# SS2D softplus in a four-layer network: the sum of its two parts moved from GpSimd to TensorE and ScalarE

## The chip, the cores and the metric

The kernel runs on one core of a Trainium2 chip. The time is the device time of one execution in microseconds; the median over several runs counts. The engines are TensorE (PE, with its weight loads as PEld), VectorE (DVE), ScalarE (ACT), GpSimd (POOL) and SyncE (SP), whose queue issues most DMAs.

## The reference

The input is an image batch of 8 x 56 x 56 x 128 in float32. Four layers follow one another. Layers 0, 2 and 3 are deformable convolutions with an MLP. Layer 1 is a state-space block (SS2D): layer norm, an input projection to 256 channels and a gate, a depthwise 3 x 3 convolution with SiLU, then a selective scan over the pixels in four directions, whose outputs are summed, normalized, gated, projected back, and followed by an MLP. The part that matters here, cut from the reference:

```python
x_dbl = jnp.einsum('bkdl,kcd->bkcl', xs, x_proj_w)
dts, Bsm, Csm = jnp.split(x_dbl, [R, R + N], axis=2)
dt = jnp.einsum('bkrl,kdr->bkdl', dts, dt_projs_w)
dt = jax.nn.softplus(dt + dt_projs_b[None, :, :, None])
A = -jnp.exp(A_logs).reshape(K, Di, N)
def step(h, t):
    dt_t, u_t, B_t, C_t = t
    h = h * jnp.exp(dt_t[..., None] * A) + (dt_t * u_t)[..., None] * B_t[:, :, None, :]
    y = jnp.einsum('bkdn,bkn->bkd', h, C_t)
    return (h, y)
```

So for each image, each of the K = 4 directions, each of the Di = 256 channels and each of the N = 16 states, a linear recurrence runs over L = 3136 pixels. Its inputs are dt (after softplus), the product dt x u, and the rows B and C that all channels share.

## The kernel before

The whole network is one program. Only the layer `Vss` (SS2D) is touched. It takes 128 steps one after the other: 8 images x 4 directions (in the order 0, 1, 3, 2) x 4 chunks of SC = 784 pixels. Directions 1 and 3 go through the image column by column, so that their views of `xb` and `y` are strided. A step is 32 units; a unit is one scan of 128 partitions (32 channels x 4 states) over 784 pixels: 8 channel groups `cg`, each with 4 state groups `sg`.

*A unit.* ScalarE makes dA = exp(dt x A) into PSUM (`decay`, L1424; two buffers). VectorE makes u = dtu x b (L1434), or, for the last of four state groups, GpSimd makes it as `up` (L1430). VectorE scans (L1537) into one of three buffers h; GpSimd multiplies h by the row c into hc (L1542; six buffers). TensorE sums hc over states into the PSUM tile acc (L1456), and ScalarE copies acc out (L1467) every eight units. ScalarE also keeps the last column of each scan as the next chunk's start (`st`, L1540). `dtu` is one PSUM tile of two banks: TensorE copies dt x u into it by an identity matmul (`spread`, L1418) once for four units, and can do so only when the last u of the four units before has been read by VectorE.

*Preparation of the next step* (`prepare`, L1314) runs beside the units as a Python generator: each `next` emits a bit of it, at two of every four units. It projects xb to dts, B and C (L1324), and for each half h of the 256 channels: a matmul with `dt` (L1337) in two parts of SH = 392 pixels, Abs and Relu on ScalarE (L1338, L1339) into `sp` and `dd[:, 0]`, then Exp and Ln on `sp` (L1341, L1342), since softplus(x) = relu(x) + log(1 + exp(-|x|)). GpSimd adds the two (L1344) and multiplies the sum by xs into `dd[:, 1]` (L1346). SP's queue stores dd to DRAM (L1348), from where `fetch_dt` (L1364) loads it spread over partitions and `fetch_row` (L1357) loads the rows of B and C. `dd` and `sp` have one buffer each.

*The background stages* run the same way, a bit for each unit in which they get a turn: `input_stage` of the next image (whose convolution is nine matmuls into one PSUM tile, L1171, twice for each chunk of 448 pixels) and `output_stage` of finished chunks. They and `prepare` share one PSUM bank, `misc`, a pool with one buffer.

*What sets the order.* The program is emitted unit by unit in Python, and a scheduler then orders each engine's instructions by priority (order of emission) and by when it takes them to be ready. The order is fixed when the program is built; each engine executes its instructions in that order and waits on semaphores.

Of the kernel before, what the change touches and what calls it, by code (L numbers as in the profile page):

```python
# [120 lines left out]
SH = SC // 2  # L121
# [911 lines left out]
class Vss:  # L1033
# [280 lines left out]
    def prepare(self, s, k, c):  # L1314

        nc, w = self.nc, self.w
        xs = self.part(self.xb, k, c)
        dbl = self.prep.tile([XD, SC], F32, name="dbl", tag="dbl")
        s["rows"] = self.dram.tile([NST, 2 * SC], F32, name="rows", tag="rows")
        s["dd"] = self.dram.tile([DI, 2 * SC], F32, name="dds", tag="dds")  # L1320
        for b in range(2):
            ps = self.misc()
            for ch in range(NCH):
                nc.tensor.matmul(ps[:XD, :SH].rearrange("p (a b) -> p a b", b=W), lhsT=w["xproj"][:, ch, k, :], rhs=xs[:, ch, SR // 2 * b : SR // 2 * (b + 1)], start=ch == 0, stop=ch == NCH - 1)  # L1324
            yield
            nc.scalar.copy(dbl[:, SH * b : SH * (b + 1)], ps[:XD, :SH])
        nc.sync.dma_start(out=s["rows"].rearrange("n (x e) -> (n x) e", x=2), in_=dbl[RANK:])
        yield
        for h in range(NCH):
            dd = self.prep.tile([128, 2, SC], F32, name="dd", tag="dd")  # L1330
            sp = self.prep.tile([128, SC], F32, name="sp", tag="sp")

            bias = w["dt_b"][:, NCH * k + h : NCH * k + h + 1]
            for b in range(2):
                at = slice(SH * b, SH * (b + 1))
                ps = self.misc()
                nc.tensor.matmul(ps[:, :SH], lhsT=w["dt"][:, k, 128 * h : 128 * (h + 1)], rhs=dbl[:RANK, at], start=True, stop=True)  # L1337
                nc.scalar.activation(sp[:, at], ps[:, :SH], AF.Abs, bias=bias)  # L1338
                nc.scalar.activation(dd[:, 0, at], ps[:, :SH], AF.Relu, bias=bias)  # L1339
                yield  # L1340
            nc.scalar.activation(sp, sp, AF.Exp, scale=-1.0)  # L1341
            nc.scalar.activation(sp, sp, AF.Ln, bias=1.0)  # L1342
            yield
            nc.gpsimd.tensor_add(dd[:, 0], dd[:, 0], sp)  # L1344
            yield
            nc.gpsimd.tensor_mul(dd[:, 1].rearrange("p (a b) -> p a b", b=W), dd[:, 0].rearrange("p (a b) -> p a b", b=W), xs[:, h])  # L1346
            yield
            nc.sync.dma_start(out=s["dd"][128 * h : 128 * (h + 1)], in_=dd.rearrange("p x e -> p (x e)"))  # L1348
            yield
# [289 lines left out]
```

## Time and profile before

| | |
|---|---|
| median of three runs | 17851.06 us (17844.23 to 17852.9) |
| profiled execution, its own time | 17839.74 us |
| span of the profiled execution | 17838.2 us |
| busy in the span: VectorE | 15386.3 us (86%) |
| TensorE | 13881.5 us (78%) |
| GpSimd | 11758.9 us (66%) |
| ScalarE | 10928.2 us (61%) |
| granted TensorE clock, mean | 0.851 |
| SS2D's scans, first to last | 2218 to 13404 us |
| in that stretch: GpSimd busy | 10437.8 of 11185.8 us |
| VectorE, TensorE, ScalarE | 10146.8, 8894.4, 6900.0 us |

The profile is one execution. Busy time is the union of an engine's instructions; PE's ends are modelled, and one float32 matmul of the program shows as two rows. A line such as "DVE h L1537 <- POOL hc L1542" says that VectorE's instruction of line 1537, which writes h, began after an idle time that ended with GpSimd's instruction of line 1542. "x4096" is a count, and names like hc<-h,c are output<-inputs.

### The profile page before, as it was taken

The page shows a single profiled execution, that of the slowest core. Times are in us where ns is not written, and L with a number is a line of the kernel's source. Part 1 is how long each engine was busy: PE and PEld are TensorE (multiplying, and loading weights), DVE is VectorE, ACT ScalarE, POOL GpSimd, SP SyncE. Part 2 cuts the span into 40 slices and gives each one's busy share as a digit, 9 for nine tenths or more (in the row PEclk, how much of TensorE's full clock was granted, in tenths as well). Part 3 has the DMA queues.
Part 4 walks back from the last instruction along what each step waited for, and adds up shares of the span by engine and source line. Part 5 has one row for each costly group of instructions (what it writes and reads, how often), then busy time and mean ns, then how long its engine had stood idle before and what let it go on. Part 6 is the DMA issues. An engine that isn't in the chain of part 4 may idle for free. (4 is left out here: it accounts for less than half of the span.)

```text
span 17838.2 us, 255485 instructions
## 1 busy us (share of the span) xinstructions
PE 13881.5 (78%) x90058; PEld 6881.4 (39%) x90058; DVE 15386.3 (86%) x17779; ACT 10928.2 (61%) x19607; POOL 11758.9 (66%) x6462
## 2 busy tenths in 40 slices
PE   5777788788788788788778878878776888777777
PEld 3555522232232233232223223223224666555555
DVE  8888488998998998998898899899996888888886
ACT  4666566566566566566666656656554666666666
POOL 2222189998998998998998999899992111122221
PEclk7788898899899899889888888989887888777778
DMA  7777544444343343343444344344434777777777
GB/s 211 211 204 206 165 153 154 172 169 150 143 159 141 139 163 137 139 165 137 143 162 143 137 158 144 140 155 150 148 134 134 199 198 199 196 210 193 209 196 176
DMA packets 1343087, 2961.69 MB, mean 166 GB/s; under 512 B 90960, under 2 KB 893716, under 8 KB 1327420
## 3 DMA queue, kind: packets, MB, share of 16 engines
q1 hardware_dynamic: 1341788, 2945.17, 52.9%
q8 instruction: 718, 11.76, 0.3%
q14 instruction: 581, 4.76, 0.1%
HBM read 2240.63 MB, written 866.92 MB: 174 GB/s over the span
## 5 line engine op out<-in xcount | busy, mean ns | idle before, releaser
L1542 POOL TENSOR_TENSOR hc<-h,c 128x784 f32<-128x784 f32 x4096 | 7539.5, 1874 | 640.9 <-DVE h L1537 387.9
L1537 DVE TENSOR_TENSOR_SCAN h<-dA,st,u 128x784 f32<-128x784 f32 x3072 | 5579.2, 1840 | 438.9 <-ACT dA L1424 243.2
L1424 ACT ACTIVATE dA<-dt,v_A 128x784 f32<-128x784 f32 x4096 | 3741.9, 915 | 842.2 <-DVE h L1537 827.7
L1456 PE MATMUL acc<-hc,v_sum 128*32 128x392 f32 x16384 | 3148.3, 542 | 103.9 <-POOL hc L1542 103.3
L1434 DVE TENSOR_TENSOR u<-dtu,b 128x784 f32<-128x784 f32 x3072 | 2864.6, 957 | 382.5 <-PE dtu L1418 378.4
L1418 PE MATMUL dtu<-dt,ident 128*128 128x392 f32 x4096 | 2028.2, 626 | 1081.9 <-issue 833.4
L760 POOL TENSOR_TENSOR ay<-hat,om 112x756 f32<-112x756 f32 (+2 forms) x192 | 504.6, 2628 | 2848.6 <-ACT hat L751 2309.7
L1537 DVE TENSOR_TENSOR_SCAN h<-dA,st,up 128x784 f32<-128x784 f32 x1024 | 1876.7, 1833 | 232.0 <-POOL hc L1542 208.6
L1430 POOL TENSOR_TENSOR up<-dt,b 128x784 f32<-128x784 f32 x1024 | 1908.1, 1863 | 79.5 <-DVE h L1537 47.1
L845 ACT COPY st<-pt 128x448 f32<-128x448 f32 (+1 forms) x2240 | 1177.4, 542 | 1201.1 <-PE pt L843 1194.6
L812 DVE TENSOR_TENSOR win<-win,patch 112x252 f32 (+2 forms) x3456 | 1686.4, 501 | 132.2 <-POOL win L803 32.5
L1540 ACT COPY st<-h 128x1 f32<-128x1 f32 x3072 | 582.6, 190 | 1985.3 <-DVE h L1537 1976.8
L843 PE MATMUL pt<-ident,sw 112*128 112x112 f32 (+2 forms) x8960 | 1600.6, 308 | 165.6 <-DMA sw<-skew 165.5
L1456 PEld LDWEIGHTS acc<-hc,v_sum 128*32 128x32 f32 x16384 | 762.0, 116 | 2485.3 <-issue 1656.6
L1418 PEld LDWEIGHTS dtu<-dt,ident 128*128 128x128 f32 x4096 | 860.1, 230 | 2150.6 <-issue 1365.5
L803 POOL MEMSET win<- 128x1820 f32 (+2 forms) x384 | 630.0, 1647 | 1298.4 <-DMA skew<-win 1111.2
L859 PE MATMUL yps<-st,xw 128*32 128x48 f32 (+5 forms) x35840 | 1075.2, 244 | 420.7 <-ACT st L845 414.6
L843 PEld LDWEIGHTS pt<-ident,sw 112*128 112x128 f32 (+2 forms) x8960 | 1113.4, 160 | 441.0 <-issue 156.8
L809 DVE TENSOR_TENSOR patch<-ay,hat 112x756 f32<-112x756 f32 (+2 forms) x1152 | 1225.3, 1070 | 39.5 <-POOL ay L760 36.6
L859 PEld LDWEIGHTS yps<-st,xw 128*32 128x32 f32 (+2 forms) x35840 | 754.1, 125 | 849.5 <-ACT st L845 501.0
L749 ACT ACTIVATE hat<-om,taps 112x252 f32<-112x252 f32 x1280 | 758.6, 730 | 277.2 <-DVE patch L809 261.4
L1448 PE MATMUL acc<-y,ident 128*64 128x392 f32 x1536 | 599.1, 780 | 348.6 <-ACT y L1467 269.5
(193 smaller groups left out, 19827.3 us busy)
## 6 DMA issues: line engine op xcount, KB each, us to landing
dt<-dds SPq DMA_DIRECT2D x1024, 784.0 KB
b<-rows SPq DMA_DIRECT2D x512, 392.0 KB
c<-rows SPq DMA_DIRECT2D x512, 392.0 KB
dds<-dd SPq DMA_DIRECT2D x256, 784.0 KB
sw<-skew SPq DMA_DIRECT2D x224, 812.0 KB
sw<-skew SPq DMA_DIRECT2D x224, 672.0 KB
sw<-skew SPq DMA_DIRECT2D x224, 588.0 KB
skew<-win SPq DMA_DIRECT2D x128, 560.0 KB
```

What stands on the lines that cost most here:

```text
L809: nc.vector.tensor_mul(patch[:n], bcast(a, 3, KX), bcast(b, 2, KY))
L812: self.last_add = nc.vector.tensor_add(to, to, patch[:n, NCB * p : NCB * (p + 1)]).ins
L843: last = nc.tensor.transpose(ps[:m, n * g : n * (g + 1)], sw[:n, g, p : p + m], self.net.ident[:n, :n])
L845: nc.scalar.copy(st[:m], ps[:m, : G * n])
L859: self.nc.tensor.matmul(yps[CG * g : CG * (g + 1), t0:t1], lhsT=xw[:m, k + part, CG * g : CG * (g + 1)], rhs=st[:m, at + t0 : at + t1], st ...
L1418: last = nc.tensor.matmul(ps[:, b, :SH], lhsT=self.net.ident, rhs=s["dt", cg][:, 1, SH * b : SH * (b + 1)], start=True, stop=True)
L1424: nc.scalar.activation(da[:, :SC], s["dt", cg][:, 0], AF.Exp, scale=w["A"][:, k, NSG * cg + sg : NSG * cg + sg + 1])
L1430: nc.gpsimd.tensor_mul(u, s["dt", cg][:, 1], s["b", sg])
L1434: nc.vector.tensor_mul(halves[0], s["dtu", cg][:, :, :SH], halves[1])
L1456: nc.tensor.matmul(acc[r : r + TC, :SH], lhsT=w["sum"], rhs=hc[:, SH * b : SH * (b + 1)], start=False, stop=sg == NSG - 1)
L1537: nc.vector.tensor_tensor_scan(hh[:, ::step], dA[:, :SC][:, ::step], u[:, ::step], st[:, t : t + 1], ALU.mult, ALU.add)
L1542: nc.gpsimd.tensor_mul(hc, hh, s["c", sg])
```

## The change

The sum on GpSimd goes. In its place, for each of two parts of 392 pixels, TensorE adds the two tiles in the shared PSUM bank by two matmuls with the identity, and ScalarE copies the sum back over `dd[:, 0]`. The product with xs stays on GpSimd. The number of turns that `prepare` takes is the same: the turn that held the sum now holds the first part, and the second part comes in one turn with the product.

```diff
             nc.scalar.activation(sp, sp, AF.Exp, scale=-1.0)
             nc.scalar.activation(sp, sp, AF.Ln, bias=1.0)
             yield
-            nc.gpsimd.tensor_add(dd[:, 0], dd[:, 0], sp)
-            yield
+            for b in range(2):
+                at = slice(SH * b, SH * (b + 1))
+                ps = self.misc()
+                nc.tensor.matmul(ps[:, :SH], lhsT=self.net.ident, rhs=dd[:, 0, at], start=True, stop=False)
+                nc.tensor.matmul(ps[:, :SH], lhsT=self.net.ident, rhs=sp[:, at], start=False, stop=True)
+                nc.scalar.copy(dd[:, 0, at], ps[:, :SH])
+                if b == 0:
+                    yield
             nc.gpsimd.tensor_mul(dd[:, 1].rearrange("p (a b) -> p a b", b=W), dd[:, 0].rearrange("p (a b) -> p a b", b=W), xs[:, h])
             yield
```

## The prediction

> **What bounds the kernel now.** First the page's busy shares, then the busy time of each engine in stretches of one image, then the waits, then the timeline. The edit stands in the SS2D layer, whose scans run from 2218 to 13404 us of the profiled execution (11186 us); the other layers don't touch it, so the whole-span shares say little. These are six stretches of the third image, cut at first scans of steps: steps 0-2, 3-7, 8-9, 10-11, 12, 13-15 (a step has 32 scans).
>
> ```profile
> core 0: us, PE busy (x) PEld busy (x) DVE busy (x) ACT busy (x) POOL busy (x), PEclk, DMA share, GB/s
> 5040.70:5292.10 251.40, 205.90 (x834) 83.62 (x833) 239.66 (x184) 167.64 (x324) 246.60 (x138) 0.91 0.44 153
> 5292.10:5765.20 473.10, 403.38 (x1327) 140.04 (x1327) 399.42 (x330) 297.14 (x508) 410.11 (x229) 0.93 0.39 138
> 5765.20:5946.50 181.30, 152.83 (x538) 52.98 (x532) 158.77 (x116) 115.94 (x210) 165.59 (x92) 0.87 0.41 144
> 5946.50:6114.60 168.10, 120.33 (x402) 34.17 (x398) 156.38 (x114) 96.23 (x151) 167.79 (x93) 0.83 0.39 140
> 6114.60:6193.20 78.60, 41.98 (x176) 13.53 (x176) 77.53 (x57) 36.98 (x72) 72.83 (x42) 0.83 0.35 126
> 6193.20:6443.70 250.50, 198.27 (x772) 76.37 (x773) 238.75 (x176) 159.41 (x275) 244.48 (x135) 0.90 0.48 172
> ```
>
> Read POOL against the length of the stretch. In the fourth it is busy 167.79 of 168.10 us: POOL sets the time. In the first and last it is at 98%, VectorE at 95%. The fifth step holds none of the removed sums, as the same stretches with the instructions of L1344 alone tell:
>
> ```profile
> 6114.60:6193.20 78.60, 0.00 (x0) 0.83 0.35 126
> ```
>
> It is the shortest, 78.6 us against some 84 a step in the others without convolution, VectorE at 99%. So VectorE's floor is 78 to 80 us a step, and the sums are part of what lies above it. The second stretch is different: it holds the input convolution, takes 94.6 us a step, PE is at 85% and POOL at 87%.
>
> How a sum reaches the scans is seen here: POOL does the sum, two hc, one up, then the product of the preparation, and a scan waits 2.44 us because none of the three h buffers has been read by its hc.
>
> ```profile
> 5974.36 1.91 POOL L1344 TENSOR_TENSOR dd<-dd,sp 128x784 f32<-128x784 f32 x1
> ...
> 5981.67 2.28 POOL L1346 TENSOR_TENSOR dd<-dd,xb 128x784 f32<-128x784 f32 x1
> ...
> 5985.80 1.85 DVE L1537 TENSOR_TENSOR_SCAN h<-dA,st,up 128x784 f32<-128x784 f32 x1 [2.44 <-POOL hc L1542]
> ```
>
> The waits over the whole execution (us in total, times, longest):
>
> ```profile
> DVE u L1434 <- PE dtu L1418: 378.4, 154, 48.6
> DVE h L1537 <- POOL hc L1542: 287.1, 261, 3.4
> DVE h L1537 <- ACT dA L1424: 246.2, 245, 5.0
> POOL dd L1344 <- ACT sp L1342: 15.4, 3, 9.8
> ```
>
> VectorE loses 287 us to POOL, but also 246 to ScalarE and 378 to TensorE (48.6 of it before the scans), the two engines that the change loads.
>
> **The change part by part.** The rows that price it, one operation each (busy, mean ns | idle before):
>
> ```profile
> L1344 POOL TENSOR_TENSOR dd<-dd,sp 128x784 f32<-128x784 f32 x256 | 476.1, 1860 | 34.4 <-DMA b<-rows 19.0 <-ACT sp L1342 15.4
> L1346 POOL TENSOR_TENSOR dd<-dd,xb 128x784 f32<-128x784 f32 x256 | 525.6, 2053 | 10.8
> L1245 ACT COPY yc<-misc 128x392 f32<-128x392 f32 x128 | 61.6, 481 | 72.8 <-PE misc L1244 72.2
> ```
>
> and for one pair of identity matmuls of 128x392, which the trace shows as four rows, at a full and at a lowered clock:
>
> ```profile
> 5961.63 1.58 PE L1418 MATMUL dtu<-dt,ident 128*128 128x392 f32 x4
> 8001.39 2.82 PE L1418 MATMUL dtu<-dt,ident 128*128 128x392 f32 x4
> ```
>
> 1. *Removed from POOL*: 256 x 1.86 = 476 us of work. On the path is only what VectorE waits for: 287 us at most, and nothing if another wait takes its place (the third rival). No such wait stands in the step without preparation, so all of it comes from the preparation's bursts. Sums are 1.86 of 1.86 + 2.05, 47%, of a burst; in proportion 136 us would go. A wait is what a burst leaves over three buffers, so halving the burst takes more than half: between 136 and 287 I take 200. Next late after that: VectorE itself, at 95% in three of the stretches.
>
> 2. *Added to TensorE*: 512 pairs x 1.58 = 809 us (1444 at the lower clock). Where PE is at 53 to 82% it lies in PE's idle time. In the convolution steps it need not: u waits for dtu there (35.1 us in this stretch). The built program's order tells how many can hurt. Between one pair of dtu matmuls and the next, some 10 us, 38 of the 512 new pairs share the interval with three or more convolution taps; 156 stand in steps with a convolution at all. Bounds: 0 (below it only by the clock, weighed further down) and 156 x 1.58 = 246 us; nearest to the crowded intervals, I take 38 x 1.58 = 60. If PE's idle time were gone elsewhere, each of the other 356 would cost its 1.58 too, 562 us.
>
> 3. *Added to ScalarE*: 512 copies of 0.48 (the L1245 row), each waiting 72.2/128 = 0.56 for its matmul: ScalarE is held 1.04 x 512 = 535 us. Behind the copy stand the next dA and, behind that, a scan. ScalarE is at 62% (6900 of 11186 us), and 245 of 4096 dA (6%) came late. Bounds 0 (added work can't gain) and half, 268; with one in eight on the path, twice today's share since ScalarE is fuller, 64 us.
>
> 4. *New wait on POOL*: the product dd x xb now follows ScalarE's second copy; behind it stand hc and up. The sum waited for ScalarE 15.4 us in all. In the built order the second copy stands one or two dA ahead of the scan whose hc follows the product, where Ln stood before the sum. I cost it at nothing, hidden by POOL's backlog; uncovered it is 256 x 1.04 = 266 us of POOL time, still below the 476 taken away, and below nothing is excluded, since a wait can't gain.
>
> 5. *PSUM*: misc is one bank, now taken ten times a step instead of six, and from the dd matmul until the copy. Behind it wait the projections and the background stages, which have slack until the next image; PE in order is the danger, since the second pair waits for the first copy with the next dtu behind it. Counted in 2; its upper end takes this in.
>
> 6. *Moved*: the product of the second half now comes at the end of a step, not some three to six units before it, and its store on SP's queue has up to two row loads behind it. Row loads hold POOL up for 14.3 us in the whole trace. Nothing, up to 128 x 2.05 = 262 us if each product's time went on to the rows. The load of dt for that half comes nine units later.
>
> Sum: -200 + 60 + 64 = -76 us against the profiled execution (17839.7 us, span 17838.2), which lies 11 under the median of the runs, 17851.1. Forecast: 17775.
>
> One rule speaks for more. TensorE's clock follows its load here: 0.83 where PE is busy 53%, 0.93 at 85%. The Trainium skill, "TensorE: Matmul & The Clock Gate", in the part on the HAM clock gate, says that activity is what releases the throttle. By it the added matmuls would lift 0.93 towards 1; of the 7 x 403 us of PE time in convolution steps some 190 would go, an estimate from that page, more than the 60 of step 2, and the sum would be -136: 17715. I stay with the rows, since four dtu rows still took 2.82 us among scans whose mean clock is 0.89.
>
> **The rivals.**
> *TensorE becomes the bound (slower)*: in the convolution steps all 156 pairs come ahead of a dtu that VectorE waits for, +246, and these steps' share of POOL's relief (16.4 of 35.4 us of that wait in the image shown, 46%) is lost: -108. With ScalarE's 64: +202, 18053. For it: 35.1 us of waits for dtu and 85%. Against: the few crowded intervals. It decides once 86 of the 156 are exposed (200 - 64 = 136 us).
> *ScalarE's copies make dA late (slower)*: half of the 535 us: -200 + 60 + 268 = +128, 17979. For it: FIFO behind a copy that waits for PE. Against: ScalarE waits 828 us for scans ahead of dA.
> *POOL's burst still overruns three buffers (same)*: -136 + 60 + 64 = -12, 17839. For it: the product, 2.05, the larger half, stays.
> *Full relief (faster)*: 287 go and the rest is hidden: 17564. For it: the step without preparation, at 78.6. Against: that one has little background work too.
>
> **How the numbers follow.** Chances: forecast 0.40, full relief 0.14, same 0.16, TensorE 0.18, ScalarE 0.12. The forecast's own range, with its terms each a little off, is 17690 to 17815. Within 0.2% (36 us), about what a measurement can tell, lies the third rival alone: faster 0.54, same 0.16, slower 0.30. The range for 8 in 10 goes from full relief to just short of the TensorE case: 17560 to 18030, leaving out half of either end.
>
> **What would show it.** Right: stretches four to six get 2 to 3 us a step shorter with POOL under 96% and VectorE over 96%; the wait of scans for hc falls from 287 towards 90. Step 2 wrong: u's wait for dtu grows by over 150 us, in the convolution steps. Step 3 wrong: the wait for dA grows from 246 past 350. Step 4 wrong: a new row, POOL dd waiting for ScalarE's copy, over 100 us.

## The result and the profile after

The changed kernel takes 17926.12 us (median of six runs, 17919.57 to 17951.31) against 17848.71 us for the kernel before (six runs beside it, 17838.29 to 17857.72). The ratio is 1.0046, with a 95% interval of 1.0033 to 1.0059: slower by 77 us, where 76 us faster was forecast. All of it lies in the SS2D scans: they take 11269 us (2225 to 13494) instead of 11186, that is +83, and the rest of the program keeps its time within 3 us.

The page's first part for the kernel after, busy us of each engine (share of the span) and instructions:

```profile
PE 14492.8 (81%) x92106; PEld 7089.2 (40%) x92106; DVE 15359.4 (86%) x17779; ACT 11180.5 (62%) x20119; POOL 11323.2 (63%) x6206
```

GpSimd lost 436 us of work (11758.9 before), as meant. TensorE gained 611, ScalarE 252. VectorE, which does the scans, has the same work as before and ends later, so it waits more. The waits of the kernel after tell for what (us in total, times, longest):

```profile
DVE u L1440 <- PE dtu L1424: 770.9, 279, 54.1
...
DVE h L1543 <- ACT dA L1430: 206.2, 197, 5.6
...
DVE h L1543 <- POOL hc L1548: 57.2, 48, 3.8
```

The wait for GpSimd's hc fell from 287 to 57 us, the relief that was forecast. The wait for ScalarE's dA fell too, from 246 to 206. But the wait of u for dtu, TensorE's copy of dt x u, doubled from 378 to 771. The three together went from 912 to 1034, +122, and the time rose by 77.

By step, over the six images 1 to 6 (counted from 0), the dtu wait grew by 53 us an image: 25 in steps 3 to 6 and 4 in step 7, where the convolution runs, but also 12 in steps 0 to 2 and 12 in steps 13 to 15, where it doesn't. In steps 8 to 12 it stayed as it was, and there the relief shows: the wait for hc fell by 13.

The same six stretches of the third image as before (steps 0-2, 3-7, 8-9, 10-11, 12, 13-15), in the kernel after:

```profile
core 0: us, PE busy (x) PEld busy (x) DVE busy (x) ACT busy (x) POOL busy (x), PEclk, DMA share, GB/s
5084.30:5339.50 255.20, 221.29 (x869) 84.17 (x869) 240.50 (x191) 174.89 (x341) 234.48 (x131) 0.97 0.43 151
5339.50:5828.40 488.90, 439.67 (x1410) 155.02 (x1411) 397.77 (x322) 309.10 (x524) 395.78 (x221) 0.94 0.38 135
5828.40:6002.90 174.50, 154.38 (x581) 54.48 (x580) 158.38 (x117) 117.42 (x212) 156.43 (x86) 0.98 0.40 142
6002.90:6164.70 161.80, 125.77 (x436) 38.56 (x434) 155.70 (x114) 100.29 (x161) 156.95 (x87) 0.87 0.41 147
6164.70:6244.00 79.30, 48.80 (x194) 15.71 (x194) 77.72 (x58) 41.31 (x81) 75.19 (x43) 0.83 0.40 143
6244.00:6498.90 254.90, 209.44 (x807) 79.14 (x807) 238.32 (x175) 161.32 (x283) 233.58 (x129) 0.96 0.47 166
```

Read the lengths against those before. The third and fourth stretch gain 6.8 and 6.3 us. The first two lose 3.8 and 15.8, and the last, which has no convolution, loses 4.4. GpSimd is at 97% in the fourth, where it was at all but 100%, and at 92% in the first and last, where it was at 98%; TensorE is at 87 to 90% in the first three. Over six images the trace gives the same picture, mean us of a step:

| steps of an image | before | after | change, whole group |
|---|---|---|---|
| 0-2 | 84.1 | 85.6 | +4.3 |
| 3-6 | 93.7 | 97.6 | +15.6 |
| 7 | 100.5 | 96.5 | -4.0 |
| 8 | 88.7 | 89.5 | +0.8 |
| 9-11 | 86.1 | 82.4 | -11.0 |
| 12 | 78.7 | 79.4 | +0.7 |
| 13-15 | 83.7 | 85.2 | +4.5 |

That is +10.9 us an image, 87 for eight.

**What a late dtu stands behind.** The timeline of the kernel after shows it. Here, in step 1 of the third image, one half of a dtu copy is done at 5226.34 and the other half, which needs the same dt and the same PSUM tile, 4.4 us later:

```profile
5226.34 0.93 PE L1424 MATMUL dtu<-dt,ident 128*128 128x392 f32 x2 [1.55 <-DVE u L1440]
...
5227.14 1.58 PE L1262 MATMUL misc<-sg,v_outb 128*128 128x392 f32 x4
...
5228.56 1.03 PE L1264 MATMUL misc<-ident,xt 98*128 98x98 f32 x8
...
5229.43 1.51 PE L1266 MATMUL misc<-yin,v_out 128*128 128x392 f32 x4
...
5230.77 0.82 PE L1424 MATMUL dtu<-dt,ident 128*128 128x392 f32 x2
...
5231.63 0.97 DVE L1440 TENSOR_TENSOR u<-dtu,b 128x784 f32<-128x784 f32 x1 [1.61 <-PE dtu L1424]
```

Between the halves TensorE ran sixteen rows of the output stage, and VectorE lost 1.61 us. None of those matmuls is new. TensorE executes its matmuls in the order of the program; the Trainium skill, "TensorE: Matmul & The Clock Gate", in the section on what each phase of a matmul is for, says that only weight loads are pulled ahead and matmuls keep program order. These rows agree: the second half needed nothing that the first had not had, and it ran after the sixteen rows.

The trace can be counted for that. There are 1023 intervals from the end of one dtu copy to the end of the next, 11 us on average. Call one crowded if matmuls other than the copy's own kept TensorE busy for 10 us or more in it:

| | before | after |
|---|---|---|
| crowded intervals | 120 | 179 |
| of them with u waiting for dtu; us waited | 76; 232 | 160; 549 |
| all intervals with u waiting for dtu | 153 | 278 |
| u's wait for dtu within the scans, us | 330 | 717 |

Look at the stretches from the release of the dtu buffer to the late u, 862 us in all before and 1825 after. The new matmuls take just 126 us of TensorE in them. The old ones take more than before: the projection of x (L1324) 187 us for 51, the convolution (L1171) 300 for 168, the sums over states 347 for 187, three lines of the output stage (L1262 to L1266) 182 for 39. Part of that is only that there are more late stretches: for each of them the convolution and the sums take 1.1 and 1.2 us in both kernels, and the projection and the output stage have grown. TensorE stood idle for 36 us of these stretches, 9 of them until one of ScalarE's new copies ended and 1 until a load of dt landed. So neither the copies nor the loads are what dtu waits for there.

**Which intervals became late.** The old matmuls themselves can be followed from one trace to the other: the n-th row of a line and its tiles before is taken for the n-th after. Of 27652 rows within the scans, 4572 run in another interval in the changed kernel. Most of these are of the output stage and the preparation. In no_sum, the kernel below without any sum, 456 do, and sum_back, below, has the order of the changed kernel in all but 26 rows. Sorted by that, u's wait for dtu is, in us:

| intervals of the changed kernel | number | before | after |
|---|---|---|---|
| with a new matmul | 349 | 69 | 170 |
| without one, into which old rows moved | 439 | 85 | 364 |
| with neither | 235 | 175 | 183 |

Of the rise of 387 us, 279 come in intervals that hold no new matmul and got old ones from elsewhere; 101 come in those with the new ones. Where nothing came in, next to nothing changed.

### The profile page after: what moved, and what is told of

Same layout as the page of the kernel before. It is cut to its first block, busy times and chain, and to the rows that moved or that the text cites. A ratio compares the mean times of both kernels' runs of the same rounds, so it can differ in the third digit from the quotient of the medians.

```text
span 17923.7 us, 259791 instructions
## 1 busy us (share of the span) xinstructions
PE 14492.8 (81%) x92106; PEld 7089.2 (40%) x92106; DVE 15359.4 (86%) x17779; ACT 11180.5 (62%) x20119; POOL 11323.2 (63%) x6206
## 5 line engine op out<-in xcount | busy, mean ns | idle before, releaser
L1462 PE MATMUL acc<-hc,v_sum 128*32 128x392 f32 x16384 | 3263.5, 535 | 4.5 <-POOL hc L1548 4.2
L1424 PE MATMUL dtu<-dt,ident 128*128 128x392 f32 x4096 | 1879.0, 577 | 831.3 <-issue 564.3
L1424 PEld LDWEIGHTS dtu<-dt,ident 128*128 128x128 f32 x4096 | 770.2, 208 | 1839.5 <-issue 1031.2
L1171 PE MATMUL misc<-xn,v_tap 128*128 128x448 f32 x2016 | 832.5, 561 | 42.2 <-ACT xn L1208 15.4
```

The lines of the kernel that those rows point to most:

```text
L1424: last = nc.tensor.matmul(ps[:, b, :SH], lhsT=self.net.ident, rhs=s["dt", cg][:, 1, SH * b : SH * (b + 1)], start=True, stop=True)
L1462: nc.tensor.matmul(acc[r : r + TC, :SH], lhsT=w["sum"], rhs=hc[:, SH * b : SH * (b + 1)], start=False, stop=sg == NSG - 1)
```

## The experiments

Each was timed beside the kernel before. The table has the three waits of VectorE from the profiled execution (u for dtu, h for hc, h for dA), their sum, and the time.

| kernel | dtu | hc | dA | sum | median us | ratio to before, 95% |
|---|---|---|---|---|---|---|
| before | 378 | 287 | 246 | 912 | 17849 | |
| after | 771 | 57 | 206 | 1034 | 17926 | 1.0046 [1.0033, 1.0059] |
| no_sum | 363 | 104 | 183 | 649 | 17568 | 0.9845 [0.9828, 0.9861] |
| sum_back | 751 | 265 | 232 | 1248 | 18183 | 1.0193 [1.0176, 1.0210] |
| one_matmul | 714 | 93 | 238 | 1045 | 17954 | 1.0062 [1.0045, 1.0079] |
| pin_after | 801 | 113 | 230 | 1144 | 18012 | 1.0094 [1.0078, 1.0111] |
| hold_only | 622 | 362 | 304 | 1287 | 18205 | 1.0200 [1.0183, 1.0217] |
| work_only | 791 | 135 | 232 | 1158 | 18069 | 1.0124 [1.0107, 1.0141] |
| mixed_k3 | 363 | 210 | 310 | 883 | 17796 | 0.9973 [0.9960, 0.9985] |
| turn_act | 547 | 259 | 159 | 965 | 17879 | 1.0017 [1.0007, 1.0026] |
| slot30_after | 645 | 33 | 227 | 905 | 17828 | 0.9989 [0.9979, 0.9999] |
| slot30_before | 554 | 261 | 328 | 1143 | 18030 | 1.0104 [1.0087, 1.0121] |
| slot30_no_sum | 470 | 44 | 302 | 816 | 17678 | 0.9912 [0.9895, 0.9929] |
| mixed_more | 359 | 197 | 290 | 845 | 17769 | 0.9964 [0.9950, 0.9979] |

The sum of the waits tells the order of the times nearly throughout: +336 us of wait and +336 of time in sum_back, -263 and -279 in no_sum, +375 and +361 in hold_only. So these three waits are where to look.

### The two halves of the change apart

First the relief alone. The sum goes and nothing takes its place; the Ln part of softplus is left out of dd.

```diff
-            for b in range(2):
-                ...
-                nc.scalar.copy(dd[:, 0, at], ps[:, :SH])
-                if b == 0:
-                    yield
+            yield
```

> The sum is left out altogether (dd keeps only the Relu part), so neither GpSimd's sums nor TensorE's pairs nor ScalarE's copies are there: POOL's relief alone. Theory 'crowded intervals' (what costs is PE work queued between two dtu pairs, and the relief itself is real): PE's queue is as before, so the wait of u for dtu stays within 330 to 400 us of its 378, the scans' wait for hc falls from 287 to under 90, time 17550 to 17650. Rival 'freed VectorE' (VectorE, no longer held by POOL, comes to dtu earlier and waits there, with or without new matmuls): the wait for dtu rises by over 150 us and the time is 17750 to 17850.

17568 us. The relief is worth 279 us, more than the 200 taken. Three waits of VectorE in this kernel:

```profile
DVE u L1433 <- PE dtu L1417: 362.5, 138, 44.7
...
DVE h L1536 <- ACT dA L1423: 183.0, 202, 3.7
...
DVE h L1536 <- POOL hc L1541: 103.9, 107, 3.4
```

The wait for hc is 183 us shorter (at 104 it stands a little above the 90 expected), and that for dA 63. The wait for dtu stays where it was before (378), so a faster GpSimd does not bring it on. That disposes of the idea that VectorE, freed, merely runs into TensorE.

Then the added work alone: the change stays, its copies go to a part of dd that the product overwrites, and GpSimd's sum is put back.

```diff
-                nc.scalar.copy(dd[:, 0, at], ps[:, :SH])
+                nc.scalar.copy(dd[:, 1, at], ps[:, :SH])
                 if b == 0:
                     yield
+            nc.gpsimd.tensor_add(dd[:, 0], dd[:, 0], sp)
```

> The changed kernel with GpSimd's sum put back beside the pairs and copies (the copies go to the tile that the product overwrites): all of the added work, no relief. PE's queue order is that of the changed kernel. Theory 'crowded intervals': the wait for dtu stays at 650 to 800 us as in the changed kernel, the scans' wait for hc comes back to 200 to 300, time 18050 to 18200. Rival 'freed VectorE': without relief VectorE comes late to dtu and the wait for dtu is under 550 us, time 17900 to 17980.

18183 us, 336 above before. The waits:

```profile
DVE u L1441 <- PE dtu L1425: 751.1, 263, 53.3
...
DVE h L1544 <- POOL hc L1549: 264.6, 314, 4.1
DVE h L1544 <- ACT dA L1431: 232.2, 208, 5.6
```

The dtu wait of the changed kernel is there without any relief of GpSimd. With it (after against no_sum) the added work costs 358, without it 336. So the two effects nearly add up, -279 and some +350, and the result is their difference.

### How much work, or where it stands

Half of the matmuls are dropped, the second of each pair; the Ln part is left out.

```diff
-                nc.tensor.matmul(ps[:, :SH], lhsT=self.net.ident, rhs=dd[:, 0, at], start=True, stop=False)
-                nc.tensor.matmul(ps[:, :SH], lhsT=self.net.ident, rhs=sp[:, at], start=False, stop=True)
+                nc.tensor.matmul(ps[:, :SH], lhsT=self.net.ident, rhs=dd[:, 0, at], start=True, stop=True)
```

> The changed kernel with the first matmul of each pair alone (the Ln part is left out of the sum): half of TensorE's added work, all of ScalarE's copies, all of POOL's relief. In its built queue 155 intervals between two dtu pairs hold over 9.2 us of other matmuls, by the durations in the trace, against 89 before and 199 after. Theory 'crowded intervals': (155 - 89) of (199 - 89), 60%, of the rise of 392 us in the wait for dtu, so 610 us of wait and 17750 to 17830. Rival 'ScalarE and misc' (the copies and the one PSUM bank that waits for them make the cost): as the changed kernel, 17890 to 17960.

This missed what crowding by the new work asked for. With half of the matmuls it takes 17954 us, 385 above no_sum against 358 with all of them, and the dtu wait is 714, of which 552 in intervals without a new matmul. So the time of the new matmuls isn't what is paid. The time is in the range that the rival, ScalarE's copies and the bank, asked for; but TensorE stood idle for only 31 of the 1637 us before the late u of this kernel too, none of them noted as a wait for a new copy. And 4542 old rows run in another interval than before.

Next the order. The bits of the background stages and of the preparation are told to be issued after the last dtu copy.

```diff
-                next(ready, None)
+                with self.tc.issue_after(self.last_spread):
+                    next(ready, None)
...
-                advance(1)
+                with self.tc.issue_after(self.last_spread):
+                    advance(1)
```

> The changed kernel, with the matmuls of the preparation and of the background stages queued behind the last dtu pair that was emitted: the same work in another order. PE work that stands directly ahead of a dtu pair falls from about 1010 to 560 us in all, but the intervals with over 9.2 us of other matmuls stay as many (193 against 199). Theory 'crowded intervals': the wait for dtu stays over 650 us, time 17890 to 17980. Rival 'what stands directly ahead' (only the matmuls just in front of a dtu pair delay it): the wait falls by some 45%, to about 430 us, time 17580 to 17700.

18012 us: worse, by 86 us, and 32 above the range. The work is the same, and the dtu wait grew by 30 us, hc's by 56. Late dtu are thus no matter of background matmuls slipping in front of the one copy that they were emitted with; and a new order alone, without any more work, is worth as much as the whole effect of the change.

### The bank turns, the work, and ScalarE

The added work does two things to TensorE's queue: time, and four more turns of the one misc bank, each of which can make TensorE wait for ScalarE. Three kernels take these apart. First short turns: before, with the pairs and copies on 8 columns beside the sum.

```diff
+            for b in range(2):
+                at = slice(SH * b, SH * b + 8)
+                ps = self.misc()
+                nc.tensor.matmul(ps[:, :8], lhsT=self.net.ident, rhs=dd[:, 0, at], start=True, stop=False)
+                nc.tensor.matmul(ps[:, :8], lhsT=self.net.ident, rhs=sp[:, at], start=False, stop=True)
+                nc.scalar.copy(dd[:, 1, at], ps[:, :8])
+                if b == 0:
+                    yield
             nc.gpsimd.tensor_add(dd[:, 0], dd[:, 0], sp)
-            yield
```

> The kernel before, GpSimd's sum included, with the pairs and copies added at 8 columns in place of 392, their result unused: four more turns of the misc bank a step, with next to no work for TensorE and ScalarE. Theory 'turns' (what costs is that the bank changes hands ten times a step in place of six, which bunches the old matmuls ahead of dtu pairs): the wait of u for dtu rises from 378 to over 600 us, time 18020 to 18150. Rival 'work' (the time that TensorE and ScalarE spend on the pairs): the wait stays under 450 us, time 17840 to 17920.

18205 us, above both ranges: as dear as full-width pairs. By the dtu wait of 622 it sided with the turns. But the groups of this kernel say that it isn't a test of turns alone; a row of 8 columns takes

```profile
L1347 PE MATMUL misc<-dd,ident 128*128 128x8 f32 x1024 | 210.6, 278 | 148.0 <-ACT dd L1349 49.3 <-ACT dd L1339 35.2 <-DVE yc L1253 26.0
```

278 ns against 561 for 392 columns in the kernel after, so TensorE's busy time still rose by 524 us (14405.4 from 13881.5), not so far from the 611 of the change.

The counterpart is work without new turns: two identity matmuls of 392 columns into the bank ahead of the dt matmul in the turn that is already there, and one more copy by ScalarE, beside the sum.

```diff
+                for _ in range(2):
+                    nc.tensor.matmul(ps[:, :SH], lhsT=self.net.ident, rhs=xs[:, h, SR // 2 * b : SR // 2 * (b + 1)], start=True, stop=True)
...
+                nc.scalar.copy(dd[:, 1, at], ps[:, :SH])
```

> The kernel before, GpSimd's sum included, with as many added matmuls (1024 of 128x392 with the identity) and copies (512 of 128x392) as the change has, their result unused, inside the turns of the misc bank that the preparation takes anyway: all of the work, no more turns. Theory 'turns': the wait of u for dtu stays under 480 us, time 17850 to 17950. Rival 'work': the wait is 650 to 800 us as with the pairs, time 18080 to 18200.

18069 us, +225, a little under the range of "work", dtu wait 791. New turns are therefore not needed for a late dtu. But this isn't the change's work in other turns. The added rows read xs and take 723 ns in the mean, for 561 and 515 in the two lines of the change, so it is the largest addition to TensorE's busy time (+916 us). And they stand in 515 of the 1023 intervals; these took 325 of the rise of 408 us within the scans. Here the added work stands in the late intervals itself, where in the changed kernel it is mostly old work. Yet the kernel costs less than sum_back and hold_only; its wait for hc fell to 135, and why isn't shown.

Last, turns without TensorE: ScalarE writes 8 columns into the bank and copies them out, four times a step, and the sum stays.

```diff
+            for b in range(2):
+                ps = self.misc()
+                nc.scalar.copy(ps[:, :8], sp[:, SH * b : SH * b + 8])
+                nc.scalar.copy(dd[:, 1, SH * b : SH * b + 8], ps[:, :8])
+                if b == 0:
+                    yield
             nc.gpsimd.tensor_add(dd[:, 0], dd[:, 0], sp)
-            yield
```

> The kernel before, GpSimd's sum included, with four more turns of the misc bank a step in which ScalarE alone writes 8 columns and copies them out again, their result unused: no instruction more for TensorE. PE's built queue is still another one: 129 intervals between two dtu pairs hold over 9.2 us of other matmuls, against 89 before and 199 with the pairs. Theory 'queue order' (the turns reorder the old matmuls, and the crowded intervals make dtu late): 40 of 110 of the rise of 392 us, a wait of u for dtu of 480 to 580 us, time 17940 to 18060. Rival 'TensorE rows' (each added matmul row costs its fixed time, however few its columns): the wait stays under 430 us, time 17840 to 17900.

17879 us, +29: the turns by themselves cost next to nothing. The dtu wait of 547 came as the theory of the queue's order had it, the time as its rival had it: 87 us less waiting for dA and 28 less for hc made up for most of the rise. The theory that the bank's turns are what is paid falls with the time. The order theory does not: without one matmul more, 3554 old rows run in another interval, and of the 169 us more of dtu wait 154 are in intervals into which they moved.

### Another place for the preparation

The preparation gets its turns at the second and third of every four units. Here it gets them at the last and the first, in the kernels after, before and without the sum (the last leaves the Ln part out).

```diff
-            if t >= 16 if early else sg in (1, 2):
+            if t >= 16 if early else sg in (3, 0):
```

> The changed kernel with the preparation's turns at the state groups 3 and 0 in place of 1 and 2: the same work and the same turns, placed after the unit that emits the dtu pair. 148 intervals with over 9.2 us of other matmuls against 199; directly ahead of dtu pairs stand 1133 us in place of 1012. Theory 'queue order': the wait of u for dtu falls from 771 to 580 to 680 us, time 17780 to 17880. Rival 'directly ahead': the wait rises, time over 17920.

> The kernel before with the preparation's turns at the state groups 3 and 0: the control for the run with the change. 99 crowded intervals against 89. Theory 'queue order': the wait of u for dtu 350 to 430 us, time 17820 to 17920. Rival 'place' (the turns' place as such decides, by what GpSimd or ScalarE do then): more than 100 us to either side of 17848.

> The preparation's turns at the state groups 3 and 0 and no sum at all (dd keeps only the Relu part): POOL's relief alone in the other order, the control for the two runs with these turns. The change's cost apart from the relief was 17926 - 17568 = 358 us in the first order. Theory 'queue order' (the same added work costs what its place in the queue makes of it): the relief is again about 280 us, time 17700 to 17800, so that the added work costs 30 to 130 us here. Rival 'work' (the added work has one price): 17430 to 17520.

With these turns the change makes the kernel faster: 18029.7 before, 17828.4 after, -201 us. With the old ones it is +77. Neither part kept its size. The relief is worth 352 us here (18029.7 - 17678.0) instead of 279, and the added work costs 150 (17828.4 - 17678.0) instead of 358; taken each against the kernel before that was timed beside it, they are 333 and 132. The changed kernel came as "queue order" expected, in wait and time. The one without the sum is 22 us below its range, and the expectation for the kernel before missed: the place of the turns alone costs it 180 us over the 17849.5 beside it. Its waits:

```profile
DVE u L1434 <- PE dtu L1418: 553.8, 284, 48.0
...
DVE h L1537 <- ACT dA L1424: 327.5, 241, 6.9
...
DVE h L1537 <- POOL hc L1542: 261.3, 206, 4.3
```

The program has no new work at all and waits 175 us more for dtu and 81 more for dA. And by the count above it has 128 crowded intervals, hardly more than the 120 before, with 506 us of dtu wait within the scans. So the number of crowded intervals goes with the change itself, but isn't a general rule. The moved rows fit here too: only 1267 run in another interval, but the 360 intervals that got some waited 336 us for 106 before, and all others 170 for 224.

### Only where it gains

By the table of steps the change gains in step 7 and steps 9 to 11. Steps 7 to 10 prepare the four steps of direction 3, step 11 the first of direction 2. First the change for direction 3 alone, GpSimd's sum elsewhere:

```diff
-            nc.gpsimd.tensor_add(dd[:, 0], dd[:, 0], sp)
-            yield
+            if k == 3:
+                for b in range(2):
+                    ...
+            else:
+                nc.gpsimd.tensor_add(dd[:, 0], dd[:, 0], sp)
+                yield
```

> TensorE and ScalarE make the sum in the steps of direction 3 alone, GpSimd in the other three quarters. There the background is thin: against the kernel before, the changed one was 12.9 us shorter in steps 9 to 11 of the third image and longer in nearly all others. Both theories: the gain of these steps stays and the loss of the others goes, 7 x 13 + 17 (last image) = 107 us less than before, 17700 to 17790. Rival 'shifted' (the scheduler moves the background elsewhere when these steps change): 17820 to 17900.

17796 us, 48 below the 17844 beside it, six over the range. Step 11 takes 87.2 us, where the fully changed kernel takes 80.5. So the first step of direction 2 was added:

```diff
-            if k == 3:
+            if k == 3 or k == 2 and c == NSC - 1:
```

> As the run with TensorE's sum for direction 3 alone, and for the first chunk of direction 2 too, whose preparation runs in the last step of direction 3. That step took 87.2 us there (mean of six images), 81.8 before and 80.5 with the change everywhere. Theory: it comes down to some 81, 8 x 6 = 48 us less than 17796: 17720 to 17775. Rival (the burst of the transition moves on to the next step): within 20 us of 17796.

17769 us (17759 to 17778), as expected, 62 below the 17831 beside it, ratio 0.9964 [0.9950, 0.9979]; step 11 is down to 81.8. The waits of this kernel:

```profile
DVE u L1444 <- PE dtu L1428: 358.6, 160, 48.0
...
DVE h L1547 <- ACT dA L1434: 289.7, 263, 5.0
...
DVE h L1547 <- POOL hc L1552: 196.6, 200, 3.5
```

The dtu wait is that of before, 90 us of the hc wait are gone and 44 of dA wait came, with the change in 5 of 16 steps. Only 1194 old rows run in another interval. It leaves out nothing and is faster than both kernels.

## Why the prediction was right and wrong, point by point

**1, relief of GpSimd: right, sized low.** 200 us taken, 230 off the wait in the kernel after, 279 of time when it stands alone. Of these 279 only 183 are off the wait for hc; 63 are off the wait for dA, which the step did not count. GpSimd then waits for VectorE 692 us, for 388 before; VectorE is the next limit, as said. The row of the waits before:

```profile
POOL hc L1542 <- DVE h L1537: 387.9, 389, 5.2
```

and two of the kernel after:

```profile
POOL hc L1548 <- DVE h L1543: 692.4, 611, 8.2
...
POOL dd L1352 <- ACT dd L1349: 29.8, 35, 2.8
```

**2, matmuls on TensorE: this is the step that failed.** It was put at +60 with 246 at most; u's wait for dtu grew by 392, and the time that the added work cost is 336 to 358 (sum_back, and after against no_sum). The mechanism was missed: the step priced only the new pairs, each by its own time, and put it at nothing that the old matmuls might change places. For that it gave no reason. The intervals with new matmuls waited 101 us more, against its 60; those that only got old rows waited 279 more. Half of the matmuls cost the same (one_matmul), an order changed by four turns of ScalarE raised the dtu wait by 169 with no matmul more (turn_act), and the same work in other turns cost 150 instead of 358 (slot30). "Where PE is at 53 to 82% it lies in PE's idle time" was wrong too, since in steps 0 to 2 and 13 to 15 the dtu wait grew by 12 us each an image and each group lost 4 us. The case named beside it, "If PE's idle time were gone elsewhere", was not carried into the sum. What should have been compared is the built order before and after. The built program's order gives 89 intervals with over 9.2 us of other matmuls between two dtu copies before, and 199 after. That count could be had before the run; the prediction counted only new pairs beside taps.

**3, copies on ScalarE: sized high.** +64 was taken for one in eight of 535 us, which is 67, and the wait for dA fell by 40. Part of that fall is the relief's: in no_sum the wait was 183, so against that kernel the change adds 23, and in sum_back, without relief, it is 14 below before. ScalarE did stand behind its copies, as this row of the groups of the kernel after shows, 0.46 us for each:

```profile
L1349 ACT COPY dd<-misc 128x392 f32<-128x392 f32 x512 | 247.2, 483 | 235.1 <-PE misc L1348 231.3
```

It had time for that, as the rival's counter-argument said: waiting for scans ahead of dA took 607 us after and 828 before.

**4, the new wait on GpSimd: right.** The product waited 29.8 us for ScalarE's second copy, in the second row above; nothing was charged, and 100 was the mark.

**5, PSUM:** the turns alone cost 29 us of time, so there was no large term to add; but they changed the order, as said under 2. **6, the product moved: right.** The product waited once for a row load, 23.3 us; the sum had waited once, 19.0.

**The clock: right direction, no gain seen.** The granted clock rose from 0.89 to 0.93 over the scans and from 0.87 to 0.98 in the third stretch, and one row of dtu went from 626 to 577 ns. That is the direction that the Trainium skill, "TensorE: Matmul & The Clock Gate", gives in the part on the HAM clock gate: activity releases the throttle. Load alone does not set the clock in these rows: before, the third stretch had 0.87 with TensorE busy 84%, the last 0.90 with 79%. The forecast by that page was 17715, and the time went the other way; how much the higher clock saved, no run separates.

**The rivals and the signs.** Of the cases, TensorE as the bound (18053) is the nearest in kind: dtu was late. Its place and price differ: it put 246 us, the new pairs' own time, into the convolution steps and let half the relief go, while the relief came in full, and the cost, some 350 us, is mostly that of moved old work and is spread over more steps. Of the signs named, "u's wait for dtu grows by over 150 us" came true, though only some 29 of 53 us an image "in the convolution steps"; the wait for hc fell below 90; stretch four got 3 us a step shorter, with GpSimd at 97% and not under 96, five and six did not. That the time lies in the range for 8 in 10 is the width of the range: both terms were low, and their errors partly cancelled.

**What stays open.** The scheduler's order changes with every edit, and with it both terms. Late dtu come where old rows moved in, in the changed kernel and in slot30_before alike; but in no_sum 103 intervals got rows and waited no longer, and in mixed_more 249 did, with 47 us for 45. Which moves make dtu late wasn't settled, nor why the scheduler made them. The built count of intervals with over 9.2 us goes with the dtu wait in most kernels (before 89, turn_act 129, slot30_after 148, one_matmul 155, pin_after 193, after 199), but not in slot30_before (99). The added work in exactly the order of the kernel before wasn't tried.

## What to carry to other kernels

Taking work off the engine that others waited for paid 279 us here for 476 us of work, but the price of the work's new place was set mostly by the order of that engine's queue, not by its idle share or the work's length. Where a scheduler orders the queues, compare the built order before and after: what stands between two of the operations that the pacing engine waits for, old work included. In these kernels that count was a warning and not a forecast of the time. And read the result by steps: used only in the steps where it gained, this change is worth 62 us instead of costing 77.

## What the runs showed of the hardware that was not expected

In these kernels a float32 identity matmul row of 8 columns took 278 ns in the mean, half of one of 392 columns in the same place (561), so narrowing it by 49 times halved it. The mean granted clock of the kernel with the 8-column pairs was 0.852, that of the kernel before (0.851), while with the full-width pairs it was 0.878.
